# Expert weights of the second layer read from SBUF by a TensorE register, a new order of pieces, and a branch hint

## The chip, the cores and the metric

The kernel runs on one core of a Trainium2 chip. A core has the engines PE (TensorE, matmuls), ACT (ScalarE), DVE (VectorE), POOL (GpSimd) and SP (SyncE), which each run their own instructions in order and wait for one another through semaphores, and 16 DMA engines that move data between HBM and the on-chip memory (SBUF). The metric is the device time of one execution in microseconds. Three runs of the kernel before took 1170.53, 1171.77 and 1175.14 us, so the median is 1171.77 us.

## The reference

The kernel computes a transformer-like stack of two layers on x of shape (4, 1024, 256), which is 4096 tokens of 256 numbers in float32. Each layer has two halves, and each half normalises x, scales and shifts it by a modulation, computes something, and adds the result back with a gate:

```
h = layernorm(x) * (1 + ca) + sa
x = x + ga * attn(h)
h = layernorm(x) * (1 + cb) + sb
x = x + gb * ffn(h)
```

In layer 0, `attn` is a bilinear attention without softmax, and `ffn` a mixture of 8 experts (256 to 1024 to 256, with ReLU) of which each token uses its best two. In layer 1, `attn` is a fast-weight MLP that walks over 8 chunks of 128 positions and lets its weights decay by the loss of each chunk:

```
out = (silu(h @ a0) * (h @ a2)) @ a1
loss = mean((out - h) ** 2);  a0, a1, a2 *= 1 - 0.001 * loss
```

The `ffn` of layer 1, where most of the change lies, is again a choice of two out of 8 experts for each token, but an expert is one matrix of 256 x 256:

```
probs = softmax(x @ router_w.T);  topk_vals, topk_idx = top_k(probs, 2)
out = sum over the two of (x @ expert_weights[idx] + probs[idx]) * weight[idx]
```

## The kernel before

**Layer 0.** x stays in SBUF as `x_sb` (128 positions, 8 chunks, 4 batches, 256). The experts' work is sorted: each (token, expert) pair gets a slot, slots are grouped by expert into blocks of 128 rows, and a block is gathered from DRAM by an indirect DMA on POOL (`gather`, L348), turned by PE (`pm_x`), multiplied by its expert's weights (`p_h` L1610, `p_y` L1633), given its bias on DVE (`y`, L1644) and stored by SP. There is room for 71 blocks (`g0.J`). The first 68 (`passed`) always run. The last three are needed only when the router's choice fills more blocks than that, and stand under `tc.If(filled > passed)` at L1855. They were not needed in these runs. The main loop does 60 blocks, and the last eight of the 68 are planned together with the first work of layer 1: the combination and the normalisation of chunks 0 and 1 (`firsts`, whose Newton iteration for the inverse root is the chain `ln_t`, `ln_y`, L1507 to L1509 on DVE).

**Layer 1.** For each chunk c: `combine` gathers the results of layer 0's experts (POOL) and adds them to `x_sb`; `normal` makes `h`, and its transpose `hT` (PE `pm_t` L1572, ACT L1581); `fast` is the MLP. Its first half is 8 steps m, each two rows of four matmuls (`p_u`, L1890, one row for `a0`, one for `a2`), a silu on ACT and a product on DVE that give `hf`. Its second half `p_f` (L1938) comes in two halves of four matmuls for each of 4 batches b. Then come a second `normal`, and `routed`, the router (`pm_l`, L2030) with the choice of the best two on DVE.

The experts of layer 1 are run in three parts. Chunks 0 to 3 form group `ga` (39 blocks), chunks 4 to 6 group `gb` (31 blocks), and chunk 7 multiplies all its tokens by all 8 experts (`dense`, `p_e` at L2251), for which the weights of all experts, `ew`, lie in SBUF since layer 0. A group is closed when its last chunk is routed. `closed` runs a chain over PE, ACT and DVE: `pm_turn` (L440), totals, `close`, `pm_blocks` (L665, `across`), `list_experts` (which writes `wrow`, the place of each block's expert in DRAM), `limits`. Then `block` runs for each block:

- DVE and PE find the rows (`reach`, `look` with `pm_counts` L739, `find`), and POOL gathers them into `xg` (ring of 4);
- SP reads `wrow` of the block into a register (L2178) and starts the transfer of 256 KB of weights into `we` (L2179, ring of 4);
- PE turns `xg` (`pm_x`, L2184), ACT copies it to `xT` (L2190), PE multiplies (`p_e`, L2203, two float32 matmuls that run as four instructions), ACT copies the result to `y` (L2213), and SP stores it to DRAM (L2216), as `ga_y` or `gb_y`.

When all blocks of a group are stored, `combine` with kind `yg2` gathers two rows per token from there, adds them and the weights' biases to `x_sb` (DVE L1462 to L1467), and the chunk is written to `out`.

**The order.** All of this is written as pieces, `plan(engine, us, do, after, holds, rank, lag)`. `Plan.run` (L61) is a list scheduler that runs once, when the kernel is built: it walks through time with the pieces' given costs, starts the ready piece of the lowest rank on each free engine if its ring slots (`holds`) are free, keeps an engine free for a soon ready piece of a clearly lower rank (`GRACE`, `PATIENCE`), and then emits the instructions in the order found. `tc.manual_schedule` keeps that order on each engine. So a changed rank or cost moves instructions on all engines, and the DMAs that they issue. The ranks that the change touches: `p_f` of chunk c has c + 0.5 + 0.1 b (L1930), `closed` c + 0.6 (L2361), `routed` and `dense` of chunk 7 have 7.38 and 8.31 (L2342, L2343), dense's DVE pieces an offset of −0.3 (L2290), and the combination of `ga` starts at 7.23 (L2387).

Of the kernel before, what the change touches and what calls it, by code (L numbers as in the profile page):

```python
# [19 lines left out]
P = 128  # L20
# [3 lines left out]
E = 8  # L24
# [113 lines left out]
def adaln_d2_kernel(  # L138
# [31 lines left out]
    def psum(pool, shape, name):  # L170
        tag = {id(ps_1): "p1", id(ps_2): "p2", id(ps_m): "pm"}[id(pool)]
        t = pool.tile([P, 512], F32, tag=tag, name=name)
        n = 1
        for s in shape[1:]:
            n *= s
        v = t[: shape[0], :n]
        if len(shape) == 3:
            v = v.rearrange("p (a b) -> p a b", b=shape[2])
        return v
# [180 lines left out]
    class Pairs:  # L360
# [353 lines left out]
        def list_experts(self):  # L714

            nc.vector.tensor_scalar(
                self.wrow, self.pb[:, 0, :], float(P), None, ALU.mult
            )

        def reach(self, scratch, j):  # L720
# [670 lines left out]
    for j in range(g0.J - SPARE, g0.J):  # L1391
# [12 lines left out]
        hT1=2,  # L1404
        hT2=2,
        hf=10,
        we=4,
        xg=4,
        xT=3,
        y=3,  # L1410
# [12 lines left out]
    def buf(kind, shape):  # L1423
        return (home[kind] if kind in home else late).tile(
            shape, F32, tag=kind, name=kind, bufs=room1[kind]
        )
# [376 lines left out]
    def late_values(j, hids, after):  # L1803
        key = ("b", j)
        at = float(j - turning)
        p2, ys = plan.slot("p2"), plan.slot("y")

        def mm():
            made[key, "p2"] = values(j, made[key, "hid"])

        def out_():
            made[key, "y"] = biased(j, made[key, "p2"])

        v = plan(PE, 3.55, mm, after=after, holds=[p2, hids], rank=at + 1.5)
        d = plan(DVE, 0.45, out_, after=[v], holds=[p2, ys], rank=at)
        of_block["kept", j] = plan(
            SP, 0.1, lambda: kept(j, made[key, "y"]), after=[d], holds=[ys], rank=at, lag=2.2
        )
        return [d]

    made[("b", turning - 1), "hid"] = hid
    hids = plan.slot("hid")
    plan("BEFORE", 0.0, lambda: None, holds=[hids], rank=-9.0)
    of_block[turning - 1] = {}
# [11 lines left out]
    for c in range(FIRST // B):  # L1836
# [12 lines left out]
        firsts[c] = normal(  # L1849
            ("n1", c), c, "1", [[d] for d in sums], (SHA, SCA), 50.0 + c, [range(B)]  # L1850
        )
    with tc.manual_schedule(engines=ORDERED | {EngineType.SP}):
        filled = nc.values_load(g0.filled[:1, :1], min_val=0, max_val=g0.J)
        plan.run()
    with tc.If(filled > passed, preferred_fallthrough_block=False):  # L1855
        for j in range(passed, g0.J):
            g0.find(work, g0.look(ps_m, g0.reach(work, j)), j)
            g0.fetch(xgbuf[j % 4], h_rows, j)
        for j in range(passed, g0.J):
            weights_in(j)  # L1860
            weights_out(j)
            xT = rows_turned(turn_rows(j))
            hid = new_hidden()
            for m4 in range(2):
                rectified(j, hid, hidden(j, xT, m4), m4)
            kept(j, biased(j, values(j, hid)))
# [5 lines left out]
    plan = Plan(rings=RINGS, **room1)  # L1872
    home["tiny"] = late
    decays = {0: ones[:, :1]}

    def fast(c, slot, slotT, ts, before):

# [49 lines left out]
        sums, squares = [], []  # L1927
        for b in range(B):
            ps = plan.slot("p2")
            rank = c + 0.5 + 0.1 * b  # L1930
            last = []
            for half in range(2):

                def mm(b=b, half=half):
                    if half == 0:
                        made[key, "p2", b] = psum(ps_2, [P, D], "p2_f")
                    for m in range(4 * half, 4 * half + 4):
                        nc.tensor.matmul(  # L1938
                            made[key, "p2", b],
                            lhsT=made[key, m][:, b * P : (b + 1) * P],  # L1940
                            rhs=a1[:, m, :],
                            start=(m == 0),
                            stop=(m == KH - 1),
                        )

                use = hids[4 * half : 4 * half + 4]
                last = [
                    plan(
                        PE,
                        1.74,  # L1950
                        mm,
                        after=[*last, *(d for d, _ in use)],
                        holds=[ps, *(h for _, h in use)],
                        rank=rank + 0.05 * half,
                    )
                ]

            def diff(b=b):
                t = made[key, "diff", b] = tiny([P, D], "diff")
                nc.vector.scalar_tensor_tensor(  # L1960
                    t,
                    made[key, "p2", b],
                    decays[c],
                    made["n1", c, "h"][:, b, :],
                    ALU.mult,
                    ALU.subtract,
                )

            def square(b=b):
                if b == 0:  # L1970
                    made[key, "loss"] = tiny([P, B], "loss")
                t = made[key, "diff", b]
                nc.scalar.activation(
                    t, t, AF.Square, accum_out=made[key, "loss"][:, b : b + 1]
                )

            def step(b=b):
                t = tiny([P, D], "step")
                nc.vector.scalar_tensor_tensor(  # L1979
                    t, made[key, "p2", b], decays[c], mods1[GA][:, b, :], ALU.mult, ALU.mult  # L1980
                )
                made[key, "step", b] = t

            def add(b=b):
                xs = x_sb[:, c, b, :]
                nc.gpsimd.tensor_tensor(xs, xs, made[key, "step", b], ALU.add)  # L1986

            df, st = plan.slot("diff"), plan.slot("step")
            d = plan(
                DVE, 0.5, diff, after=[*last, *before], holds=[ps, slot, df], rank=rank - 0.6  # L1990
            )
            squares.append(plan(ACT, 0.6, square, after=[d], holds=[df], rank=rank - 0.6))
            d = plan(
                DVE, 0.5, step, after=[*last, d], holds=[ps, st], rank=rank - 0.55
            )
            sums.append(plan(POOL, 0.75, add, after=[d], holds=[st], rank=rank - 0.55))
# [151 lines left out]
    def block(g, j, rows, y, lists, experts, stored, rank):  # L2148
# [18 lines left out]
            holds=[look],  # L2167
            rank=rank - 0.4,
        )
        xg, we, ps, xTs = plan.slot("xg"), plan.slot("we"), plan.slot("pm"), plan.slot("xT")  # L2170

        def fetch():
            made[key, "xg"] = buf("xg", [P, D])
            g.fetch(made[key, "xg"], rows, j)

        def weights():
            made[key, "we"] = buf("we", [P, KD * D])
            at = nc.sync.value_load(g.wrow[:1, j : j + 1], min_val=0, max_val=(E - 1) * P)  # L2178
            nc.sync.dma_start(made[key, "we"], ew_in[bass.ds(at, P), :])  # L2179

        def turn():
            pt = made[key, "pt"] = psum(ps_m, [P, KD, P], "pm_x")
            for k in range(KD):
                nc.tensor.transpose(  # L2184
                    pt[:, k, :], made[key, "xg"][:, k * P : (k + 1) * P], ident
                )
# [2 lines left out]
            made[key, "xT"] = buf("xT", [P, KD, P])  # L2189
            nc.scalar.copy(made[key, "xT"], made[key, "pt"])  # L2190

        w = plan(SP, 0.5, weights, after=[experts], holds=[we], rank=rank - 0.3)
        w = moved(0.95, [w], rank - 0.3, [we])
        f = plan(POOL, 1.28, fetch, after=[f, *stored], holds=[xg], rank=rank - 0.3)
        f = moved(0.5, [f], rank - 0.35, [xg], 1.0)
        m = plan(PE, 0.28, turn, after=[f], holds=[xg, ps], rank=rank - 0.2)
        a = plan(ACT, 0.45, turned_, after=[m], holds=[ps, xTs], rank=rank - 0.2)
        p2, ys = plan.slot("p2"), plan.slot("y")

        def mm():  # L2200
            made[key, "p2"] = psum(ps_2, [P, D], "p2_e")
            for k in range(KD):
                nc.tensor.matmul(  # L2203
                    made[key, "p2"],
                    lhsT=made[key, "xT"][:, k, :],
                    rhs=made[key, "we"][:, k * D : (k + 1) * D],
                    start=(k == 0),
                    stop=(k == KD - 1),
                )
# [5 lines left out]
        def store():  # L2215
            nc.sync.dma_start(y[j * P : (j + 1) * P, :], made[key, "y"])  # L2216

        m = plan(PE, 0.87, mm, after=[a, w], holds=[we, xTs, p2], rank=rank)
        a = plan(ACT, 0.45, out_, after=[m], holds=[p2, ys], rank=rank - 0.2)
        s = plan(SP, 0.35, store, after=[a], holds=[ys], rank=rank - 0.2)  # L2220
        return moved(0.5, [s], rank - 0.4, [ys], 1.6)
# [1 line left out]
    def dense(c, slotT, ts, d, x, rank):  # L2223
# [19 lines left out]
        for b in range(B):  # L2243
            last, st = [], plan.slot("step")
            for j in range(E // 2):
# [13 lines left out]
                def out_(b=b, j=j):  # L2259
# [3 lines left out]
                    for i in range(2):  # L2263
# [23 lines left out]
                        out_,  # L2287
                        after=[m, x, *last],
                        holds=[ps, st],
                        rank=rank + 0.1 * b + 0.02 * j - 0.3,  # L2290
                    )
                ]

# [20 lines left out]
    for c in range(NC):  # L2314
# [24 lines left out]
        )  # L2339
        which = 0 if c < 4 else 1  # L2340
        if c == NC - 1:
            d, x = routed(last_pairs, c, 0, slotT, ts, 7.38)  # L2342
            dense(c, slotT, ts, d, x, 8.31)  # L2343
            continue
        g, first = groups[which], 4 * which
        at = (c - first) * B
# [11 lines left out]
            plan(SP, 0.1, store, after=hs, holds=[slot], rank=c + 1.1, lag=3.5)  # L2358
        )
        if c in (3, 6):  # L2360
            lists, experts, slots = closed(g, lasts[which], c + 0.6)  # L2361
            base, span = ([4.57, 1.5], [7.35, 0.66])[which]
            ys = [
                block(
# [11 lines left out]
            for q in range(first, c + 1):  # L2376
# [7 lines left out]
                    vbs[which],  # L2384
                    mods1[GB],
                    [*ys, slots],
                    (7.23, 7.89)[which] + 0.2 * (q - first),  # L2387
                )

                def store(q=q):  # L2390
# [65 lines left out]
```

## Time and profile before

The profile is of one execution that took 1148.51 us, 23 us less than the median of the runs; its span is 1146.5 us. All spans and windows below are of that execution.

| what | value |
|---|---|
| median of the runs (lowest, highest) | 1171.77 us (1170.53, 1175.14) |
| the profiled execution, its span | 1148.51 us, 1146.5 us |
| mean granted PE clock over the span | 0.988 |
| layer 0 with its eight planned blocks ends, layer 1's first `p_u` starts | 636.66 us |
| `p_u` (512), `p_f` (512) busy | 230.3 us, 115.3 us |
| `p_e` of the blocks (280) busy, mean of one | 73.2 us, 393 ns |
| transfers of `we`: number, KB each, median to landing | 70, 256.0, 3.8 us |
| stores of `ga_y` (39) and `gb_y` (31): median to landing | 3.3 us, 4.7 us |
| gathers of `xg` for gb (31): POOL busy each, median to landing | 0.95 us, 4.7 us |
| bytes moved by all DMA queues | 140.50 MB |
| first and last gather of gb start | 1033.4 us, 1085.3 us |
| last block's `p_e` ends, last DVE instruction ends | 1102.97 us, 1141.80 us |

How to read it: the profile's parts are busy times of engines, groups of instructions by source line, waits (which engine at which line stood idle, and what released it), the chain of work that ended last, and tables by time window. A row such as "PE p_e L2203 <- DMA we<-in_ew" means that PE's matmul into `p_e` at line 2203 waited for the transfer that writes `we` from the DRAM input `in_ew`. `x280` counts instructions, PE is matmul and PEld the weight load that overlaps it; a "q" behind an engine's name is its sequencer, which loads registers, computes addresses and branches. The granted clock is the share of full TensorE speed that the chip allowed.

### The profile page before, as it was taken

The page shows a single profiled execution, that of the slowest core. Times are in us where ns is not written, and L with a number is a line of the kernel's source. Part 1 is how long each engine was busy: PE and PEld are TensorE (multiplying, and loading weights), DVE is VectorE, ACT ScalarE, POOL GpSimd, SP SyncE. Part 2 cuts the span into 40 slices and gives each one's busy share as a digit, 9 for nine tenths or more (in the row PEclk, how much of TensorE's full clock was granted, in tenths as well). Part 3 has the DMA queues.
Part 4 walks back from the last instruction along what each step waited for, and adds up shares of the span by engine and source line. Part 5 has one row for each costly group of instructions (what it writes and reads, how often), then busy time and mean ns, then how long its engine had stood idle before and what let it go on. Part 6 is the DMA issues. An engine that isn't in the chain of part 4 may idle for free. (4 is left out here: it accounts for less than half of the span.)

```text
span 1146.5 us, 18577 instructions
## 1 busy us (share of the span) xinstructions
PE 1101.7 (96%) x6244; PEld 873.2 (76%) x6244; DVE 589.4 (51%) x2243; ACT 428.2 (37%) x1156; POOL 413.8 (36%) x479
## 2 busy tenths in 40 slices
PE   9999899999999999999998999999999999999894
PEld 5997799999999999999988565665666676646651
DVE  7686332322122222222237598877677535787567
ACT  5967233323333322333325333423325325333321
POOL 2000334433443343334355452420125232536535
PEclk8999999999999999999999999999999999999988
DMA  9303423656441514242162221200028564337944
GB/s 341 121 23 111 140 83 102 218 170 202 133 153 37 190 38 152 74 152 80 38 216 71 74 65 47 65 19 19 0 78 245 167 169 137 102 99 214 283 131 142
DMA packets 88388, 140.50 MB, mean 123 GB/s; under 512 B 24730, under 2 KB 63136, under 8 KB 83684
## 3 DMA queue, kind: packets, MB, share of 16 engines
q0 software_dynamic: 31680, 69.61, 20.0%
q1 hardware_dynamic: 55508, 68.10, 18.5%
q10 hardware_dynamic: 1104, 1.58, 0.4%
q8 instruction: 51, 0.84, 0.3%
q14 instruction: 45, 0.37, 0.1%
HBM read 222.48 MB, written 30.57 MB: 221 GB/s over the span
## 5 line engine op out<-in xcount | busy, mean ns | idle before, releaser
L1622 ACT ACTIVATE hid<-p_h,w 128x128 f32<-128x128 f32 x544 | 154.9, 368 | 324.6 <-issue 263.7
L1610 PEld LDWEIGHTS p_h<-xT,w 128*128 128x128 f32 x2176 | 252.9, 192 | 7.8 <-DVE xT L1595 3.9
L1610 PE MATMUL p_h<-xT,w 128*128 128x128 f32 x2176 | 254.5, 275 | 4.0 <-DVE xT L1595 4.0
L1633 PE MATMUL p_y<-w,hid 128*128 128x256 f32 x1088 | 248.9, 382 | 0.0
L1890 PE MATMUL p_u<-hT,a 128*128 128x512 f32 x512 | 230.3, 596 | 2.4 <-ACT hf L1902 1.5
L348 POOL DMA_INDIRECT w<-in_W,g_wrow x134 | 133.8, 999 | 263.9 <-ACT hid L1622 121.4
L1633 PEld LDWEIGHTS p_y<-w,hid 128*128 128x128 f32 x1088 | 201.6, 190 | 24.6
L1890 PEld LDWEIGHTS p_u<-hT,a 128*128 128x128 f32 x512 | 93.8, 190 | 101.3 <-issue 89.9
L1595 DVE COPY xT<-pm_x 128x256 f32<-128x256 f32 x68 | 28.8, 424 | 177.0 <-PE pm_x L1590 176.8
L1644 DVE TENSOR_TENSOR y<-p_y,w 128x256 f32<-128x256 f32 x68 | 28.8, 424 | 172.1 <-PE p_y L1633 172.1
L1938 PE MATMUL p_f<-a,hf 128*128 128x256 f32 x512 | 115.3, 380 | 0.0
L348 POOL DMA_INDIRECT xg<-h_rows,g_row x68 | 65.7, 966 | 129.6 <-DVE g_hits L752 109.1
L1938 PEld LDWEIGHTS p_f<-a,hf 128*128 128x128 f32 x512 | 96.3, 190 | 15.5 <-issue 2.9
L348 POOL DMA_INDIRECT yg<-y,g_slot x64 | 61.5, 961 | 83.6 <-DVE x_sb L1467 45.2
L2203 PE MATMUL p_e<-we,xT 128*128 128x256 f32 x280 | 73.2, 393 | 4.1 <-DMA we<-in_ew 3.5
L1902 ACT ACTIVATE hf<-p_u,decay 128x512 f32<-128x512 f32 x56 | 38.1, 683 | 67.6 <-PE p_u L1890 65.1
L2203 PEld LDWEIGHTS p_e<-we,xT 128*128 128x128 f32 x280 | 50.1, 194 | 14.7 <-issue 5.5
L1986 POOL TENSOR_TENSOR x_sb<-x_sb,step 128x256 f32<-128x256 f32 x32 | 24.2, 758 | 99.3 <-DVE step L1979 87.5
L348 POOL DMA_INDIRECT xg<-ga_rows,ga_row x39 | 37.1, 950 | 53.2 <-DVE g_hits L752 19.4
L1530 DVE TENSOR_TENSOR h<-h,mod 128x256 f32<-128x256 f32 x128 | 50.9, 422 | 5.8 <-ACT h L1520 3.4
L1906 DVE SCALAR_TENSOR_TENSOR hf<-p_u,decay,hf 128x512 f32<-128x512 f32 x56 | 41.9, 748 | 17.2 <-PE p_u L1890 13.5
L2213 ACT COPY y<-p_e 128x256 f32<-128x256 f32 x70 | 25.8, 371 | 60.1 <-PE p_e L2203 27.2
(368 smaller groups left out, 1295.7 us busy)
## 6 DMA issues: line engine op xcount, KB each, us to landing
we<-in_ew SPq DMA_DIRECT2D x70, 256.0 KB, 3.8
y<-y SPq DMA_DIRECT2D x68, 128.0 KB, 1.8
ga_y<-y SPq DMA_DIRECT2D x39, 128.0 KB, 3.3
x_sb<-in_x SPq DMA_DIRECT2D x8, 512.0 KB
h_rows<-h SPq DMA_DIRECT2D x8, 512.0 KB, 3.6
gb_y<-y SPq DMA_DIRECT2D x31, 128.0 KB, 4.7
out_x<-x_sb SPq DMA_DIRECT2D x7, 512.0 KB, 3.1
a<-in_fw SPq DMA_DIRECT2D x6, 512.0 KB
```

Source lines behind the costliest of these rows:

```text
L348: return nc.gpsimd.indirect_dma_start(out=dst, out_offset=None, in_=table, in_offset=bass.IndirectOffsetOnAxis(ap=index, axis=0), bounds_c ...
L1530: nc.vector.tensor_tensor(h, h, mods1[(sc, sh)[i]][:, b, :], (ALU.mult, ALU.add)[i])
L1595: nc.vector.tensor_copy(xT, pt)
L1610: nc.tensor.matmul(p1[:, i, :], lhsT=w1[:, k * H + m * P : k * H + (m + 1) * P], rhs=xT[:, k, :], start=(k == 0), stop=(k == KD - 1),)
L1622: nc.scalar.activation(hid[:, m, :], p1[:, i, :], AF.Relu, bias=w1buf[j % 2][:, KD * H + m : KD * H + m + 1],)
L1633: nc.tensor.matmul(p2, lhsT=hid[:, m, :], rhs=w2[:, m * D : (m + 1) * D], start=(m == 0), stop=(m == KH - 1),)
L1644: nc.vector.tensor_tensor(y, p2, w2buf[j % 2][:, KH * D :], ALU.add)
L1890: nc.tensor.matmul(pu, lhsT=a[:, k, m * P : (m + 1) * P], rhs=made["n1", c, "hT"][:, k, :, :], start=(k == 0), stop=(k == KD - 1),)
L1902: nc.scalar.activation(made[key, m], made[key, m, 0], AF.Silu, scale=decays[c])
L1906: nc.vector.scalar_tensor_tensor(h, made[key, m, 1], decays[c], h, ALU.mult, ALU.mult)
L1938: nc.tensor.matmul(made[key, "p2", b], lhsT=made[key, m][:, b * P : (b + 1) * P], rhs=a1[:, m, :], start=(m == 0), stop=(m == KH - 1),)
L2203: nc.tensor.matmul(made[key, "p2"], lhsT=made[key, "xT"][:, k, :], rhs=made[key, "we"][:, k * D : (k + 1) * D], start=(k == 0), stop=(k == ...
```

## The change

Three parts.

1. **Weights from SBUF.** `weights()` and the ring `we` are gone. `wrow` now holds the offset of the expert in the free dimension of `ew` (expert times KD·D = 512) instead of a DRAM row. `turn` loads it into a register of PE, and the second operand of each matmul in `mm` is a slice of `ew_flat` (the same SBUF tile `ew`, seen flat) that starts at that register plus k·D. PE's `turn` now waits for `list_experts`.
2. **The order.** Ranks: `p_f` c + 0.5 to c + 0.37, `closed` c + 0.6 to c + 0.97, dense's DVE offset −0.3 to −0.5, `routed` of chunk 7 7.38 to 7.46, `dense` 8.31 to 8.23, ga's combination 7.23 to 6.49. With the pieces of `weights` gone, the scheduler finds another order in layer 1 anyway.
3. **The branch.** Before the last block's `p_y`, a new piece `expected` closes the written order, adds a branch hint (likely taken) to PE for the label "late", and opens the written order again. The `If` gets that label, and `preferred_fallthrough_block` goes from False to True: the three extra blocks are laid out directly behind the branch, and the path on which they aren't needed is reached by a taken branch.

```diff
         def list_experts(self):
             nc.vector.tensor_scalar(
-                self.wrow, self.pb[:, 0, :], float(P), None, ALU.mult
+                self.wrow, self.pb[:, 0, :], float(KD * D), None, ALU.mult
             )
...
-        we=4,
...
+        if j == passed - 1:
+            plan(PE, 0.05, expected, after=after, rank=at + 1.4)
         v = plan(PE, 3.55, mm, after=after, holds=[p2, hids], rank=at + 1.5)
...
+    def expected():
+
+        ordered.close()
+        before = [i for i in nc.cur_bb.bb.instructions if i.engine == EngineType.PE][-1]
+        tc.mark_branch_hint_location("late", "LikelyTaken", [EngineType.PE])
+        tc.add_manual_dep(
+            nc.cur_bb.bb.instructions[-1],
+            before.name,
+            mybir.DependencyInfo(mybir.DependencyClass.NoSync, mybir.DependencyReason.DATA),
+        )
+        ordered.enter_context(tc.manual_schedule(engines=ORDERED | {EngineType.SP}))
...
-    with tc.manual_schedule(engines=ORDERED | {EngineType.SP}):
+    with ExitStack() as ordered:
+        ordered.enter_context(tc.manual_schedule(engines=ORDERED | {EngineType.SP}))
         filled = nc.values_load(g0.filled[:1, :1], min_val=0, max_val=g0.J)
         plan.run()
-    with tc.If(filled > passed, preferred_fallthrough_block=False):
+    with tc.If(filled > passed, preferred_fallthrough_block=True, label="late"):
...
+    ew_flat = ew.rearrange("p e k o -> p (e k o)")
...
-            rank = c + 0.5 + 0.1 * b
+            rank = c + 0.37 + 0.1 * b
...
-        def weights():
-            made[key, "we"] = buf("we", [P, KD * D])
-            at = nc.sync.value_load(g.wrow[:1, j : j + 1], min_val=0, max_val=(E - 1) * P)
-            nc.sync.dma_start(made[key, "we"], ew_in[bass.ds(at, P), :])
-
         def turn():
+            made[key, "at"] = nc.tensor.value_load(
+                g.wrow[:1, j : j + 1], min_val=0, max_val=(E - 1) * KD * D
+            )
...
-        w = plan(SP, 0.5, weights, after=[experts], holds=[we], rank=rank - 0.3)
-        w = moved(0.95, [w], rank - 0.3, [we])
...
-        m = plan(PE, 0.28, turn, after=[f], holds=[xg, ps], rank=rank - 0.2)
+        m = plan(PE, 0.28, turn, after=[f, experts], holds=[xg, ps], rank=rank - 0.2)
...
-                    rhs=made[key, "we"][:, k * D : (k + 1) * D],
+                    rhs=ew_flat[:, bass.ds(made[key, "at"] + k * D, D)],
...
-        m = plan(PE, 0.87, mm, after=[a, w], holds=[we, xTs, p2], rank=rank)
+        m = plan(PE, 0.87, mm, after=[a], holds=[xTs, p2], rank=rank)
...
-                        rank=rank + 0.1 * b + 0.02 * j - 0.3,
+                        rank=rank + 0.1 * b + 0.02 * j - 0.5,
...
-            d, x = routed(last_pairs, c, 0, slotT, ts, 7.38)
-            dense(c, slotT, ts, d, x, 8.31)
+            d, x = routed(last_pairs, c, 0, slotT, ts, 7.46)
+            dense(c, slotT, ts, d, x, 8.23)
...
-            lists, experts, slots = closed(g, lasts[which], c + 0.6)
+            lists, experts, slots = closed(g, lasts[which], c + 0.97)
...
-                    (7.23, 7.89)[which] + 0.2 * (q - first),
+                    (6.49, 7.89)[which] + 0.2 * (q - first),
```

More of the change, by code (lines that the diff above doesn't have):

```diff
@@ L2169, in block @@
         )
-        xg, we, ps, xTs = plan.slot("xg"), plan.slot("we"), plan.slot("pm"), plan.slot("xT")
+        xg, ps, xTs = plan.slot("xg"), plan.slot("pm"), plan.slot("xT")
         def fetch():
```

## The prediction

> **What bounds the kernel now.** First the page's busy row and the windows by stage (columns: window; length; then busy us and instructions of PE, PEld, DVE, ACT, POOL; granted clock; DMA share; GB/s).
>
> ```profile
> PE 1101.7 (96%) x6244; PEld 873.2 (76%) x6244; DVE 589.4 (51%) x2243; ACT 428.2 (37%) x1156; POOL 413.8 (36%) x479
> 636.66:858.00 221.34, 220.22 (x779) 134.08 (x780) 173.15 (x584) 74.92 (x158) 64.16 (x71) 1.00 0.15 45
> 858.00:960.00 102.00, 99.36 (x451) 69.96 (x449) 54.95 (x233) 41.09 (x112) 37.32 (x41) 1.00 0.67 186
> 960.00:1031.10 71.10, 68.86 (x246) 40.37 (x246) 56.52 (x188) 28.36 (x60) 32.26 (x34) 1.00 0.34 106
> 1031.10:1102.97 71.87, 63.47 (x319) 49.60 (x318) 41.89 (x193) 27.02 (x78) 34.37 (x37) 0.95 0.79 233
> 1102.97:1141.80 38.83, 26.47 (x61) 10.75 (x59) 34.30 (x85) 7.57 (x13) 24.42 (x24) 0.93 0.41 126
> ```
>
> PE is the bound nearly everywhere: no matmul goes away, so the change can win only PE's idle time and slow clock. Before 636.66 (layer 0) it touches almost nothing. Layer 1's three middle stages leave PE 1.12, 2.64 and 2.24 us idle; the fourth, in which the 31 blocks of gb run, 71.87 − 63.47 = 8.40 us, and it alone has a clock under 1 (0.95) and the busiest DMA (0.79). Then the waits there, the chain, and PE's timeline:
>
> ```profile
> PE pm_x L2184 <- DMA xg<-gb_rows,gb_row: 4.2, 4, 1.4
> PE p_e L2203 <- DMA we<-in_ew: 3.5, 4, 1.4
> 1085.08 6.98 DMA we<-in_ew
> 1086.64 1.10 PE L2203 MATMUL p_e<-we,xT 128*128 128x256 f32 x4
> 1089.17 2.04 PE L2203 MATMUL p_e<-we,xT 128*128 128x256 f32 x4 [1.43 <-DMA we<-in_ew]
> 1092.20 2.04 PE L2203 MATMUL p_e<-we,xT 128*128 128x256 f32 x4 [0.56 <-DMA we<-in_ew]
> 1094.03 1.60 PE L1572 MATMUL pm_t<-ident,h 128*128 128x128 f32 x8
> ```
>
> The weights' transfer, 256 KB a block, takes up to 6.98 us (median 3.8), holds p_e up, and shares DMA with the gathers of xg (median 4.7 us to landing here), which hold pm_x up. After two such waits the same four p_e last 2.04 us instead of 1.10.
>
> **Part 1, weights from SBUF.** It removes 70 transfers of 256 KB (17.9 of 140.5 MB) and, on SP, each block's load of the index (0.27 + 0.15 + 0.02 us) and SP's wait for a free `we` slot, behind which y's stores queue. Gain in the gb stage: idle 8.40, plus the slow clock: two p_e of 2.04 against 1.10 (1.9), pm_t 1.60 against 1.04 at 1014 (0.6), a pm_x pair 0.63 against 0.39 (0.2) = 2.7. Together 11.1. The waits on we vanish; those on xg shrink, for the transfer of each block falls from 512 KB (we, xg, y) to 256; they don't vanish. I leave 2.3 idle: **+8.8**. Bounds: 4 (only 3.3 of we-waits, and part of the clock) to 11.1.
>
> It adds on PE's queue, per block, a register load, its checks and one address calculation before each of two matmults. PE's trace has a single such load:
>
> ```profile
> L2178 SPq TENSOR_LOAD <-gb_wrow x31: 266/269/727, 1028.1 to 1093.3; - x31
> L1853 PEldq TENSOR_LOAD <-g_filled x1: 482/482/482, 563.7 to 563.7; - x1
> 563.84 3.67 PE L1633 MATMUL p_y<-w,hid 128*128 128x256 f32 x16
> ```
>
> SP's load costs 0.27, PE's 0.48 us (SP's own load of that tile took 0.476, so it is perhaps the tile that costs more, not the engine). Add 0.15 (SP's regops), 0.02, and 2 × 0.04 (SP's address calculation): 0.52 to 0.73 us of sequencer time a block. It lies beside PE's execution if the sequencer runs ahead: at 563.7 it loaded while 16 matmuls of p_y (3.67 us) were still to execute, and PE did not idle. A block executes for 0.22 (pm_x) + 0.06 (pm_counts) + 0.87 (p_e) = 1.15 us; its 14 instructions take at most 27 ns each to issue (pm_turn's weight-and-matmul pairs stand 0.055 us apart at 1022.15), 0.38, so 0.90 to 1.11 with the load: just under 1.15. In ga, rows of p_u (1.74 us per 4 matmuls) lie between blocks. The load stands ahead of the transposes that wait for xg, so it runs before that wait. Cost: nothing to 70 × 0.52 = 36; I take **−0.5**, near the observed load, with some exposed after a long wait.
>
> The expert index must now be there for the turn on PE, not for SP: queued behind it is all of PE. It is written before the limits which every block's count already needs, so this wait costs 0.
>
> **Part 2, the order.** PE's order shows: closed() of gb starts later, and two more rows of p_u (or p_f in their place), 3.45 us, are ahead of the first count. That covers two waits that stand bare now:
>
> ```profile
> PE pm_blocks L665 <- DVE g_diagonal L657: 1.2, 1, 1.2
> PE pm_turn L440 <- DVE ga_both L432: 1.0, 1, 1.0
> ```
>
> The 3.45 us isn't lost (the rows move, they aren't added), but gb's first gather comes 3.45 − 1.2 = 2.25 us later, near 1035.7. POOL has 31 gathers × 1.25 (0.95 + 0.30 of issue) + 4 adds × 1.06 = 43 us to do, then a landing of 4.7 and 1.5 for turn, copy and p_e: 1085 at the earliest, before the 1094 that 1102.97 − 8.8 gives. So POOL isn't the bound. The four xg slots: held 0.95 + 4.7 + 0.5 = 6.2 us each, 1.54 a block, 31 in 48: 1085 again; at a landing of 6.0 (the longest now) 58 us, 1095. That is rival B. Gains: **+1.2** (pm_blocks) and, in ga, **+1.0** (pm_turn). p_f moves its first four matmults of a chunk ahead of the last p_u row; b1's half still stands between hf 7 and its reader (1.74 + 1.74 us against ACT 0.68 + DVE 0.75), so no new wait; of the other small waits of 858 to 1031 (3.9 − 1.0 for turn, 1.2 for blocks: 2.7 left) perhaps **+0.5**. Ten instead of four blocks stand behind chunk 7's turn, so chunk 7's router and shares are finished before the end; DVE's dense part can start at once: **+0.5** at most, for in the last window DVE is busy 34.30 of 38.83 and POOL's gathers alternate with it.
>
> One thing moves the wrong way. Closing the written order at block 66 puts DVE's y of that block ahead of chunk 1's root chain, where DVE, in order, waits for p_y:
>
> ```profile
> 630.62 0.42 DVE L1644 TENSOR_TENSOR y<-p_y,w 128x256 f32<-128x256 f32 x1 [0.40 <-PE p_y L1633]
> 636.66 13.57 PE L1890 MATMUL p_u<-hT,a 128*128 128x512 f32 x31 [0.85 <-ACTq L1855]
> ```
>
> Now the chain (ln_t) starts at 626.40 and y waits at 630.62. After, the chain starts at 631.0, ends 1.93 later, and h (four ACT of 0.52, eight DVE of 0.42 behind), then pm_t, then ACT's four hT copies (2.05 in all) follow. Part of the 4.6 us has slack (pm_t waited for p_y of block 67); from rows: last pm_t 634.8 becomes 636.8, so p_u starts at 638.65: **−2.0** (0 to −4).
>
> **Part 3, hint and blocks of the If.** The PE gap there is 0.85 us, and what ends it is ACT's queue (its copies end 636.56, then its branch), not PE's branch: a hint for PE alone gains 0 (at most 0.85). [...] The path run here is now the taken one, on every engine, unhinted on ACT. Rows: the compares cost 0.04 to 0.30 us, with no stall, but not taken. [...] **0**, low end −1.8.
>
> **Sum** in the profiled execution (1148.51 us, span 1146.5): 8.8 + 1.2 + 1.0 + 0.5 + 0.5 − 0.5 − 2.0 = **+9.5**, so 1139.0. The runs shown have a median of 1171.77, 23.3 above that execution; the gain is carried over unscaled: **1162.3**.
>
> **Rivals.**
> A, *SBUF weights cost PE more than they bring* (slower). Place: PE's sequencer between two blocks; each pair of transposes waits for its gather, which may empty the queue so that the next load lies bare. Price 0.52 us × 70 = 36 at most; it decides from 10/70 = 0.14 a block. At two thirds (0.35): 1162.3 + 24 = **1186**. For: gb's blocks stand back to back, with 1.11 against 1.15. Against: the load at 563.7, beside matmuls under way. 0.07.
> B, *the gathers rule anyway*. First gather 2.25 later and landings that stay at 6: T0 1098 instead of 1094, and the L0 loss at its worse end: gain 3.5, **1168**. For: xg's waits (4.2) were already more than we's (3.5). Against: half the bytes go. 0.18.
> C, *all idle and slow clock go*: 11.1 + 2.2 + 1.5 + 1.5 of the tail, L0 loss 0.5: +16, **1156**. 0.20.
> D, *the new block order costs its fetch* (1.8, perhaps twice) with the rest as forecast: 1164 to 1166; 0.08. Forecast: 0.47, own range 1158 to 1166.
>
> Range 1151 to 1170: it takes in B, C, D and most of the bounds above (4 instead of 8.8 in the gb stage gives 1167), and leaves A out. A measurement here tells about 0.5% (5.9 us) from no change: faster holds C, D's better half and nearly all of the forecast (0.76); same B and the rest (0.17); slower A (0.07).
>
> **What would show it.** In the changed profile: no wait on we, PE idle in the gb stage under 3 us with clock 1.00; pm_x's waits on xg under 2; PE's load of wrow lying under busy PE (idle "issue" on p_e under 1 us in all); no pm_blocks or pm_turn wait; DVE's y of block 66 idle some 4 us before p_y, and p_u starting near 638.7. Wrong: p_e or pm_x idle in 0.2 to 0.5 us portions at each block (A), long pm_x waits on xg (B), p_u starting after 640 (D).

## The result, and the profile after

The changed kernel takes 1162.08 us (median of 7 runs, 1161.22 to 1164.23) against 1170.53 us for the kernel before (1168.75 to 1175.14): a ratio of 0.9924 with a 95% interval of 0.9904 to 0.9945, so by the ratio 8.9 us faster (8.45 by the two medians), where 9.5 was forecast. A second set of runs gave 0.9923 (0.9907 to 0.9939).

The two profiles don't show this as they stand. The changed kernel's profiled execution has a span of 1160.3 us, 13.8 *longer* than the one of before (1146.5). The execution of before is not typical: its kernel's median is 22 us above it. (Its 1148.51 us lie among those that chip C gives for this kernel, 1148.17 to 1155.88, and its trace looks like those of chip C; see the last section.) The kernel before was therefore profiled again (run b_again below), and that profile, with a span of 1163.6 us, is what "before" means from here on, unless said otherwise.

Windows by stage of the second profile of before (layer 1 up to gb's first count; the gb stage up to the end of the last block's `p_e`; the rest), columns as in the prediction:

```profile
643.78:1040.42 396.64, 388.96 (x1474) 244.53 (x1475) 284.56 (x1004) 143.97 (x328) 133.74 (x145) 1.00 0.32 92
1040.42:1117.66 77.24, 65.68 (x319) 50.28 (x318) 42.06 (x192) 26.70 (x78) 34.61 (x37) 0.96 0.75 216
1117.66:1163.60 45.94, 28.11 (x60) 11.21 (x59) 34.27 (x85) 7.56 (x13) 24.36 (x24) 0.87 0.38 118
```

The same three stages of the changed kernel:

```profile
646.83:1047.64 400.81, 392.46 (x1485) 246.54 (x1486) 284.98 (x1002) 144.39 (x329) 134.90 (x147) 1.00 0.22 67
1047.64:1113.00 65.36, 57.98 (x307) 44.89 (x306) 40.24 (x204) 25.98 (x77) 32.45 (x35) 1.00 0.44 123
1113.00:1160.30 47.30, 27.74 (x61) 11.56 (x59) 32.49 (x75) 7.57 (x13) 23.67 (x24) 0.86 0.37 115
```

The gb stage is 11.9 us shorter (77.24 to 65.36), its clock is at 1.00 where it was 0.96, and its DMA share fell from 0.75 to 0.44. Some of this is work that moved: four matmuls of `p_u` and eight of `p_f`, the 3.45 us of the prediction, now stand ahead of the first count, and the stage ahead is 4.2 us longer. It also starts 3.0 us later. The two profiles come from different sets of runs, so their spans (3.3 us apart) don't give the gain; e2 and b_again below share a chip, and there spans (11.1) and medians (11.6) agree.

PE's idle time in the gb stage fell from 11.6 to 7.4 us, where the prediction looked for under 3. PE's waits there (sum, times, longest), in b_again:

```profile
PE p_e L2203 <- DMA we<-in_ew: 4.1, 4, 1.4
PE pm_x L2184 <- DMA xg<-gb_rows,gb_row: 0.8, 2, 0.5
```

and in the changed kernel:

```profile
PE pm_x L2198 <- issue: 2.3, 4, 1.3
PE pm_counts L739 <- ACT xT L2204: 0.8, 1, 0.8
PE pm_x L2198 <- PE pm_x L2198: 0.8, 2, 0.4
...
PE pm_x L2198 <- DMA xg<-gb_rows,gb_row: 0.8, 1, 0.8
```

No wait on weights is left. The gathers hold PE up by 0.8 us, but they did no more in b_again: the 4.2 us that the prediction hoped to shrink stand in the first profile only. About half of what remains (3.7 us) stands before `pm_x` under "issue" and under releasers other than its gather. That is the subject of the last experiment.

### The profile page after: what moved, and what is told of

Its sections match the earlier page's. It is cut to its first block, busy times and chain, and to the rows that moved or that the text cites. A ratio compares the mean times of both kernels' runs of the same rounds, so it can differ in the third digit from the quotient of the medians.

```text
span 1160.3 us, 18416 instructions
## 1 busy us (share of the span) xinstructions
PE 1109.2 (96%) x6244; PEld 875.8 (75%) x6244; DVE 586.3 (51%) x2243; ACT 427.4 (37%) x1156; POOL 412.1 (36%) x479
## 3 DMA queue, kind: packets, MB, share of 16 engines
q1 hardware_dynamic: 45428, 49.75, 12.7%
## 5 line engine op out<-in xcount | busy, mean ns | idle before, releaser
L1632 PE MATMUL p_y<-w,hid 128*128 128x256 f32 x1088 | 252.1, 384 | 3.2 <-issue 3.2
L2215 PE MATMUL p_e<-ew,xT 128*128 x280 | 70.3, 384 | 0.3 <-ACT y L2225 0.3
L2215 PEld LDWEIGHTS p_e<-ew,xT 128*128 128x128 f32 x280 | 49.5, 190 | 10.4 <-issue 4.9
```

Of the source, the lines that this page charges most:

```text
L1632: nc.tensor.matmul(p2, lhsT=hid[:, m, :], rhs=w2[:, m * D : (m + 1) * D], start=(m == 0), stop=(m == KH - 1),)
L2215: nc.tensor.matmul(made[key, "p2"], lhsT=made[key, "xT"][:, k, :], rhs=ew_flat[:, bass.ds(made[key, "at"] + k * D, D)], start=(k == 0), st ...
```

## The experiments

Each kernel was timed beside the kernel before on the same chip. The kernel before itself took 1166.4 us on chip A, 1170.8 on B and 1152.9 on C, so absolute times are compared on one chip only, and even ratios across chips with care: one kernel (e6 and e7) has 0.9879 on B and 0.9921 on C, with intervals that don't meet.

| run | chip | ratio to before (95% interval) |
|---|---|---|
| b_again: before, unchanged | A | 1.0003 (0.9987 to 1.0019) |
| e1: part 1 alone | A | 0.9995 (0.9980 to 1.0009) |
| e2: parts 1 and 2 | A | 0.9913 (0.9891 to 0.9934) |
| e3: part 3 alone | A | 1.0043 (1.0026 to 1.0060) |
| e4: part 1, order of before kept | B | 0.9977 (0.9962 to 0.9992) |
| e5: part 2 alone | B | 0.9946 (0.9928 to 0.9965) |
| e6: all but the hint's piece | B | 0.9879 (0.9861 to 0.9896) |
| after_again: the whole change | B | 0.9923 (0.9907 to 0.9939) |
| e7: as e6 | C | 0.9921 (0.9898 to 0.9944) |
| e8: e7 and a hint without a piece | C | 0.9932 (0.9913 to 0.9950) |
| e9: as e2 | C | 0.9935 (0.9914 to 0.9956) |
| e10: e7 with two loads a block | C | 1.0175 (1.0152 to 1.0198) |

Stage lengths in us, read from the matmuls' rows of each profile (first `p_u`; from there to gb's first count; from there to the end of the last block's `p_e`; from there to the end of the span; how many blocks' `pm_x` still follow chunk 7's last router matmul; when DVE's dense part starts, counted from the end of the last `p_e`; PE's idle time in the gb stage; its granted clock there):

| profile | first p_u | to count | gb stage | rest | blocks behind | dense starts | PE idle, gb | clock, gb |
|---|---|---|---|---|---|---|---|---|
| before, first profile | 636.7 | 394.5 | 71.9 | 43.5 | 1 | +1.6 | 8.4 | 0.95 |
| b_again | 643.8 | 396.6 | 77.3 | 45.9 | 1 | +1.6 | 11.6 | 0.96 |
| the whole change | 646.8 | 400.8 | 65.4 | 47.2 | 6 | −0.8 | 7.4 | 1.00 |
| e1 | 642.6 | 398.5 | 69.7 | 53.4 | 0 | +9.3 | 9.7 | 0.98 |
| e4 | 645.2 | 405.6 | 71.9 | 48.6 | 1 | +1.6 | 8.4 | 0.98 |
| e5 | 646.9 | 396.6 | 71.0 | 47.8 | 9 | −13.1 | 8.6 | 1.00 |
| e2 | 644.8 | 398.5 | 64.3 | 44.9 | 6 | −0.8 | 6.3 | 1.00 |
| e3 | 644.8 | 398.8 | 77.2 | 46.5 | 1 | +1.6 | 11.1 | 0.93 |
| e7 | 641.8 | 397.1 | 61.5 | 42.7 | 6 | −0.8 | 3.7 | 1.00 |
| e10 | 640.7 | 408.7 | 76.4 | 42.7 | 6 | −0.8 | 15.4 | 0.98 |

**b_again: the kernel before, once more.**

> The kernel before, unchanged, for a second profile. Its profiled execution of record (1148.51 us) lies 22 us below the median of its runs, and the changed kernel's profile (span 1160.3) is 13.8 us longer than it although the medians say 8.4 us shorter. If that execution was an odd one, this profile has a span near 1168 us and shows in which stage the 20 us lie (layer 0 ends near 636.7 in the odd one; later here). If profiles simply run shorter than plain runs for this kernel, the span is again near 1147. Timed: ratio 1.000 within 0.3%.

The span is 1163.6 us: the first profile was the odd one. Layer 0 ends 7.1 us later than in it and the gb stage is 5.4 us longer. What the traces show of this is told in the last section.

**e1: part 1 alone** (the diff of part 1, ranks and `If` as before).

> Before plus part 1 alone (weights from SBUF by a register of PE; ranks and If as before). My sum: +8.8 in the gb stage, +0.5 elsewhere, -0.5 of sequencer: 8 to 9 us faster, ratio 0.992 to 0.993. Rival A (sequencer exposed): slower than before, ratio 1.01 or more. Rival B (gathers rule anyway): 2 to 4 us faster, 0.997.

Measured: no difference that the interval shows (0.9980 to 1.0009). The gb stage is 7.6 us shorter, which looks like the forecast, and the rest of the kernel 7.5 us longer. But part of the 7.6 is work that moved behind the stage: chunk 7's router and four of the experts' matmuls behind it, some 3.6 us together. PE idles only 1.8 us less in it. The timeline of e1 shows what happened (PE, then DVE's first instruction of the dense part):

```profile
1108.97 1.04 PE L1571 MATMUL pm_t<-ident,h 128*128 128x128 f32 x8
1109.85 1.03 PE L2199 MATMUL p_e<-ew,xT 128*128 x4
1110.71 1.89 PE L2030 MATMUL pm_l<-rw_sb,hT 128*128 128x64 f32 x16
...
1120.16 0.54 DVE L2263 TENSOR_SCALAR step<-p_e,d_w,d_vb 128x256 f32<-128x256 f32 x1
```

and the same DVE instruction in b_again:

```profile
1119.27 0.54 DVE L2267 TENSOR_SCALAR step<-p_e,d_w,d_vb 128x256 f32<-128x256 f32 x1
```

Without the weights' pieces, the scheduler sees blocks ready earlier and puts all of them ahead of chunk 7's router (`pm_l`). DVE's choice of experts and shares, on which the dense part waits, then lies bare behind the last block: dense starts at 1120.2, and in b_again, whose blocks end 6.8 us later, at 1119.3. From there to the end both take 44 us (44.3 in b_again, 44.0 in e1). The blocks got faster and the end of the kernel didn't move.

**e4: part 1 with the order of before kept.** The pieces stay in the plan and emit nothing:

```diff
         def weights():
-            made[key, "we"] = buf("we", [P, KD * D])
-            at = nc.sync.value_load(g.wrow[:1, j : j + 1], min_val=0, max_val=(E - 1) * P)
-            nc.sync.dma_start(made[key, "we"], ew_in[bass.ds(at, P), :])
+            pass
```

> Weights from SBUF by PE's register, but the pieces of the weights stay in the plan (their transfer and SP's load are left out of the emission), so every engine keeps the order of the kernel before. Theory after the first runs: the register path itself is worth what the sum said for the gb stage (5 to 9 us there), and in the run with part 1 alone it was given back because the plan, without the weights' pieces, put chunk 7's turn and router behind all blocks but one. Then here: 6 to 9 us faster than before, ratio 0.992 to 0.995, last p_e of a block 6 to 9 us earlier after its first count, tail as long as before (46 us). Rival: the tail lengthens whenever the blocks finish earlier, because POOL's gathers and DVE's alternation set the end: ratio 0.998 to 1.000.

Measured: 2.7 us faster (0.9 to 4.4), below the forecast, above the rival. The gb stage holds the same instructions as in b_again and is 5.4 us shorter: PE idles 3.2 us less, and the clock is 0.98 for 0.96. No wait on weights is left in it, but 3.6 us of new ones (`PE p_e L2205 <- ACT y L2215`). Dense starts where it did (+1.6): with the order kept, the gain isn't given back to the router. Why only half of the 5.4 arrives at the end isn't settled. The one profile of this run is of its slowest execution (1173.31 us, median 1168.06) and loses 9 us against b_again before gb's first count, so it can't tell.

**e5: part 2 alone** (the six ranks; weights by transfer).

> The new ranks alone; weights by transfer as before, If as before. If the order is the whole gain: ratio 0.991. If the order needs the freed DMA: PE waits on we stay (3 to 6 us in the gb stage), gain 2 to 4 us, ratio 0.997; the ten blocks that then lie behind chunk 7's turn cover its router, so the tail is 2 to 4 us shorter than before.

Measured: 6.3 us faster (4.1 to 8.4), more than the second theory gave. Nine blocks now follow chunk 7's router, and dense is ready 13.1 us before the last block ends. The waits on the weights' transfers stay, smaller. PE's waits in the gb stage of e5:

```profile
PE p_e L2203 <- DMA we<-in_ew: 2.4, 4, 1.0
PE pm_x L2184 <- DVE step L1979: 1.6, 1, 1.6
```

So the order needs no free DMA to pay. And no run ties the clock to the transfers: in the gb stage it is 1.00 here, at a DMA share of 0.74, and 0.98 in e1 and e4, whose weights lie in SBUF.

**e2: parts 1 and 2 together** (ranks and weights, `If` as before).

> Before plus parts 1 and 2 (weights from SBUF and the new ranks; If as before). My sum: 8.8 + 2.7 + 0.5 - 0.5 = 11.5 us faster than before, ratio 0.990, so some 2 us faster than the whole change, because y of block 66 is not pulled ahead of the root chain. If the hint and the new layout of the If bring something, it is slower than the whole change instead.

The two parts together give 10.1 us (7.7 to 12.7), about the sum of e4 and e5 (9.0). But those two ran on chip B, and there the same two parts, in e6 below (with the new layout of the `If`), give 14.2 (12.2 to 16.3). So on B they are worth more together than apart, and what they are worth differs by chip (9.1 and 7.5 on C, by e7 and e9). The forecast had this run 2 us ahead of the whole change; by their ratios it is ahead by 1.2, which their intervals don't tell from nothing. e6 does, next.

**e3: part 3 alone**, and **e6: the whole change without the hint's piece.**

```diff
-        if j == passed - 1:
-            plan(PE, 0.05, expected, after=after, rank=at + 1.4)
```

> Before plus part 3 alone (the hint's piece, the label and the new layout of the If). My sum: 2.0 us slower (0 to 4), ratio 1.0017; the profile shows DVE's y of block 66 idle some 4 us before p_y, and the first p_u of chunk 0 some 2 us later after block 67's p_y than before. [...] If the hint pays: faster by up to 1 us.

> The whole change without the hint's piece; label and new layout of the If stay. The order of the planned part is then that of before again (y of block 66 amid the modulations). If the 5 us that part 3 cost alone come from that order: 4 to 5 us faster than the whole change, ratio to before 0.988 to 0.991. [...]

> The whole change again, on the same chip as the three others, to compare with them. Ratio 0.992 to 0.995; profile: first p_u 11.4 us after block 66's p_y starts, POOL's first gather of chunk 2 more than 2 us after the first p_u.

Part 3 alone costs 5.0 us (3.0 to 7.0), and taking the hint's piece out of the whole change wins 3.7 back: 1158.33 against 1162.04 us on the same chip, with intervals of the ratio that don't meet. The new layout of the `If` is still in e6, so the taken branch isn't what costs. DVE and POOL in b_again, then in e3:

```profile
638.14 0.42 DVE L1644 TENSOR_TENSOR y<-p_y,w 128x256 f32<-128x256 f32 x1
...
641.20 0.42 DVE L1644 TENSOR_TENSOR y<-p_y,w 128x256 f32<-128x256 f32 x1 [0.72 <-PE p_y L1633]
...
644.17 0.94 POOL L348 DMA_INDIRECT yg<-y,g_slot  x1 [9.77 <-DMA y<-y]
```

```profile
636.96 0.42 DVE L1644 TENSOR_TENSOR y<-p_y,w 128x256 f32<-128x256 f32 x1 [2.95 <-PE p_y L1633]
...
643.08 0.42 DVE L1644 TENSOR_TENSOR y<-p_y,w 128x256 f32<-128x256 f32 x1
...
644.76 24.32 PE L1905 MATMUL p_u<-hT,a 128*128 128x512 f32 x56 [0.77 <-ACTq L1870]
...
647.82 0.94 POOL L348 DMA_INDIRECT yg<-y,g_slot  x1 [13.78 <-DMA y<-y]
...
670.09 3.70 PE L1905 MATMUL p_u<-hT,a 128*128 128x512 f32 x8 [1.01 <-DVE hf L1921]
```

Count from the start of block 66's `p_y` (634.08 and 633.30 in these profiles). `p_u` starts 9.70 us later in b_again and 11.46 in e3: the 1.8 us that the stalled DVE costs directly. But block 67's y now stands behind all eight modulations of h and comes at 9.78 instead of 7.12 us; its store takes 1.8 us longer to land (last section), and POOL, which may only gather from `y` when all of it is stored, starts at 14.52 instead of 10.09. Chunk 2's combination, and with it DVE's products for `hf`, come later too, and PE waits 1.0 us for `hf` at 670.09. In the table, e3 starts `p_u` late as told and takes 2.2 us longer from there to the count; how the whole 5.0 divides is not settled by one profile.

**e7, e8, e9: the hint and the layout apart.** In e8 the hint is emitted inside the piece of block 67's y, so that only PE's instruction list differs:

```diff
         def out_():
             made[key, "y"] = biased(j, made[key, "p2"])
+            if j == passed - 1:
+                expected()
```

> The whole change without the hint's piece, again, as the common reference of the next three. Ratio 0.986 to 0.990.

> As the run before, with the hint on PE put in without a piece of its own (amid block 67's last turns), so that no other engine's order moves; the one difference is the hint. If the hint itself is worth nothing: the same within 0.2% (ratio to before 0.986 to 0.990), first p_u again 9.7 us after the start of block 66's p_y. If the hint works on the critical path: first p_u up to 0.9 us earlier. If the hint itself costs the 5 us, and not the order: 0.991 to 0.994.

> Parts 1 and 2 with the If as before (no label, not-needed path falls through), beside the new layout without the hint. If the layout is worth nothing either way: equal within 0.2%. [...] The first pair of single calls (0.9913 here, 0.9879 there) would make this one 4 us slower.

Measured on one chip: 1144.32 us without a hint, 1143.97 with it, 1144.81 with the `If` as before, all three with the same order on PE, DVE, ACT and POOL. The medians lie within 0.9 us, less than the runs of each scatter, and the first `p_u` comes 9.70 us after block 66's `p_y` in each. No worth of the hint shows, here 4.3 us ahead of PE's compare, and none of the layout in either direction. The forecast ratio of e7 (0.986 to 0.990) was missed on this chip, so e8 and e9 are compared with e7 and not with their own forecast ratios. (e2 and e6 ran on different chips; e7 and e9 are the same two kernels on one, and the 4 us between them don't come again.) Each of e2, e6, e7, e8 and e9 is faster than the kernel before; e6 is also shown to be faster than the whole change, and is the version to keep.

**e10: the register load doubled.**

```diff
+            nc.tensor.value_load(
+                g.wrow[:1, j : j + 1], min_val=0, max_val=(E - 1) * KD * D
+            )
             made[key, "at"] = nc.tensor.value_load(
```

> As e7, but PE loads each block's index twice: 0.30 + 0.15 + 0.02 = 0.47 us more of its sequencer for each of 70 blocks. If the load lies beside running matmuls: the same as e7 within 2 us (it may show in gb, where the blocks stand back to back). If rival A's mechanism is at work and just small: 0.2 to 0.47 us for each of gb's 31 blocks, so 6 to 15 us slower than e7, last p_e of gb's blocks later by as much.

Measured: 1171.52 against 1144.32 us, 27.2 us for 70 loads, 0.39 each of the 0.47 that a load takes with its checks:

```profile
L2191 PEldq FUSED_REGOPS  x70: 146/151/165, 857.5 to 1093.7; - x70
L2191 PEldq SEQ_ASSERT  x70: 18/18/24, 857.7 to 1093.9; - x70
L2191 PEldq TENSOR_LOAD <-gb_wrow x31: 294/302/705, 1041.5 to 1093.3; - x31
```

In gb it is 14.9 us for 31 blocks, all of it: there a second load has no cover at all. In ga, where rows of `p_u` lie between blocks, it is 11.6 for 39, or 0.30 each, which was not forecast. Then the first load can have little to spare. Start times of `pm_x` of consecutive blocks in e7:

```profile
1078.55 0.38 PE L2196 MATMUL pm_x<-ident,xg 128*128 128x128 f32 x2
...
1079.91 0.41 PE L2196 MATMUL pm_x<-ident,xg 128*128 128x128 f32 x2
...
1081.30 0.41 PE L2196 MATMUL pm_x<-ident,xg 128*128 128x128 f32 x2
...
1082.57 0.41 PE L2196 MATMUL pm_x<-ident,xg 128*128 128x128 f32 x2
```

and in e10:

```profile
1095.52 0.41 PE L2199 MATMUL pm_x<-ident,xg 128*128 128x128 f32 x2 [0.45 <-DVE g_hits L752]
...
1097.27 0.41 PE L2199 MATMUL pm_x<-ident,xg 128*128 128x128 f32 x2 [0.37 <-PE p_e L2216]
...
1099.08 0.41 PE L2199 MATMUL pm_x<-ident,xg 128*128 128x128 f32 x2 [0.42 <-DVE h L1529]
...
```

These blocks take 1.27 to 1.39 us in e7, where their matmuls need 1.15, and 1.75 to 1.81 in e10: the difference is the second load. In these rows of e7 the load at 1080.24, beside running weight loads, takes 0.57 us, where the middle one of gb's loads takes 0.30. But they are among the slower ones. Of gb's 13 blocks in e7 that are followed by another with nothing between, the fastest takes 1.08 us and the middle one 1.27; in b_again and e5, without a load on PE, the faster of such blocks take 1.08 to 1.20. By these times, as an estimate, one load a block is about as much as the sequencer bears; that it sets the pace in places was not shown. The releasers in brackets (DVE's `g_hits`, DVE's `h`) are the last events seen, not causes: the gap is of nearly equal size (0.37 to 0.45) whatever is named. Summed over e7, PE stands idle about 5.8 us in some 20 gaps before a `pm_x` that isn't put down to xg, and 28 us in e10. Not all of the 5.8 is the load's: by the same count the kernel before has 0.9 in its first profile and 2.8 in b_again, and e5 4.4. Loading the index a block earlier, or several at once, was not tried.

## Why the prediction was right, step by step

The time and the sign were right (1162.3 forecast, 1162.08 measured). That they agree to 0.2 us is luck: several terms were mis-sized and cancelled, and the 9.5 was taken from a median of 1171.77 that became 1170.53 with more runs.

- **The gb stage, +8.8.** The waits on weights are gone, as forecast, and PE's idle time and slow clock shrink. But the term was mis-sized for part 1: with the same instructions in the stage (e4) it is 5.4 us shorter, and 2.7 of them reach the end. The sum counted on shrinking 4.2 us of waits on xg, of which b_again has 0.8, and gave the slow clock to the transfers, while e5 has a clock of 1.00 with the transfers in place. And it took the order as given: taking pieces out of a list scheduler's plan changes the order, and by itself this lost the whole gain (e1, 0.9995).
- **Ten blocks behind chunk 7's turn, "+0.5 at most".** This was one of the most mis-sized terms. I read the ordering from the final kernel, saw a tail limited by DVE and POOL, and priced it by that tail. Part of its work is to keep the router from becoming the end once blocks are fast: in e1, without the new ranks, dense starts 7.7 us later after the last block, and the 7.5 us of its tail are lost. Part 2 alone is worth 6.3 us, where my sum gave it 1.2 + 1.0 + 0.5 + 0.5 = 3.2. Why it gains that much even with the transfers in place (gb stage 6.3 us shorter, clock 1.00) was not taken apart.
- **The covered waits and the later start.** `pm_turn`'s wait is gone from the changed profile, and so is that of gb's `pm_blocks`; ga's `pm_blocks` has one of 0.8 us in its place. On chip C, e7 reaches gb's first count 397.1 us after the first `p_u`, against 394.5 in the first profile of before: +2.6; on chip A e2 has +1.9 over b_again. 2.25 was forecast.
- **The load on PE, −0.5 (0 to −36).** The step that said 0.90 to 1.11 us of sequencer time is "just under 1.15" failed. The load itself was priced well (0.47, and 0.05 for each address). But e10's 1.78 us a block, less two loads and two addresses, leave about 0.75 for the other instructions (an estimate from these rows), where the prediction had 0.38; with one load that makes about 1.3. The row it leaned on, a load at 563.7 that hid behind 3.67 us of queued matmuls, has no like in gb: in e7 the load at 1080.24 starts when the block's first `p_e` (1080.22) has just begun. What it costs at one load a block was not isolated: at most about 5.8 us, by the gaps counted above. Rival A's mechanism shows at two loads, where 27.2 us come on top and the kernel is slower than before (1.0175).
- **Block 66's y, −2.0 (0 to −4).** The first `p_u` came 1.8 us later, as worked out. I followed the stall only along PE's next input. DVE's queue also held block 67's y, for which SP's store and POOL's gathers wait. The price was 5.0 us alone (e3), and 3.7 in the whole change (e6 against it).
- **Hint and layout, 0 (low end −1.8).** Right for both (e7 to e9). No run shows the −1.8 of the low end, nor rival D's 1.8, as a cost: the not-needed path is as fast taken (e7, 1144.32 us) as fallen through (e9, 1144.81). The compare on PE takes 0.49 us in the changed kernel, in one go, where the kernel before had two, of 0.10 and 0.30 in its first profile and of 0.10 and 0.40 in b_again.
- **Rival B** (gathers rule anyway) fell: xg holds PE up by 0.8 us only, and POOL waits 8.5 us in the stage for `pm_x` to free a slot of xg. **Rival C** (all idle time goes) fell: 7.4 us are left in the gb stage, and 3.7 in e7. **Rival D** fell with e6 and e9.

## What to carry to other kernels

Where a scheduler writes the order, a part that is removed moves everything else: test it once with its place kept and once without, or its worth can't be told from the order's. When work in front of the end gets faster, look for the chain that has to be done by then and is still placed last; here it was the router of the last chunk. A wait in an in-order queue costs what stands behind it for every other engine, not only for the next one: in e3 it was 1.8 us at PE's next input and 5.0 us in all.

## What was not expected of the hardware

**PE's signals came late, and that differs between chips.** In b_again, DVE waited 5.1 us for `xT` at a place where PE had executed the transposes and ended its last matmul by 591.78, 1.9 us before, and e1's tail has a hole of 6.5 us in which both engines stand. DVE in b_again:

```profile
593.67 0.42 DVE L1595 COPY xT<-pm_x 128x256 f32<-128x256 f32 x1 [5.13 <-remote]
```

PE and DVE in e1 ("remote": released by an event whose sender the profile doesn't know):

```profile
1133.89 1.96 PE L2247 MATMUL p_e<-ew,hT 128*128 128x512 f32 x4 [0.27 <-issue]
...
1141.56 1.00 DVE L2272 SCALAR_TENSOR_TENSOR step<-p_e,d_w,step 128x256 f32<-128x256 f32 x2 [6.50 <-remote]
...
1142.71 1.19 PE L2247 MATMUL p_e<-ew,hT 128*128 128x512 f32 x1 [6.86 <-DVE step L2272]
```

PE's last matmul ends at 1135.85; its semaphore's next update is recorded at 1141.54, and DVE starts 0.02 us later. In the profiles of chips A and B, and in the changed kernel's first, 1,158 to 1,187 updates of PE's semaphore are recorded for some 1,245 matmuls that make one. In the changed kernel's first (1,187 updates), 14 of those until the last matmul come more than 0.8 us after the end of the matmul before them, up to 2.57 us. They stand in three groups (592.4 to 593.4, 612.2 to 612.4, 1136.1 to 1136.2), each 0.9 to 2.3 us after the end of a gather on POOL. In the first profile of before (1,249 updates) and in all four of chip C, 1,245 to 1,249 are recorded and none is over 0.8 us late. The kernel before is 14 to 18 us faster on C. That the late signals are what makes the difference is likely but not shown, and what holds them was not found. With holes of 5.1 and 6.5 us in single profiles of chip A, small differences between stages of single profiles of A and B have to be read with care.

**A store behind an instruction fetch.** In e3, the store of block 67's y has sent 135 of its 144 packets by 645.05; the last nine start at 645.80. A fetch of 16 KB of instructions runs on the DMA engines from 644.45 to 645.82. The whole change shows the same twice: fetch until 647.71 and the nine from 647.71, fetch until 649.68 and the nine from 649.66. In b_again and e6 the store comes 2.7 us earlier after block 66's `p_y`, and its last packet starts before the fetch does. So the nine packets, a sixteenth of the 144, as one of the 16 DMA engines would carry, seem to stand behind the fetch; this is read from the times, no run took the fetch away. On POOL, 2.7 us of delay on DVE became 4.4 us.
